# Attention with a mixture-of-experts gate: transposing through DRAM and 32x32 blocks on VectorE in place of DMA transposes

## The chip, the cores and the metric

The kernel runs on one core of one Trainium2 chip. Its engines are TensorE (PE in the profile; PEld is its weight load), VectorE (DVE), ScalarE (ACT), GpSimd (POOL) and SyncE (SP). SP computes nothing: it only issues DMAs. ACT and POOL issue DMAs too, between their computations. Each engine runs its own instructions strictly in order, so an instruction that waits holds up everything behind it on that engine. The metric is the device time in microseconds; lower is better.

## What is computed

The input `x` is 2 x 2048 rows of 512 floats, all in float32. Cut to what matters:

```python
xn = layernorm(x)
# attention branch, causal, one head of 512
z = layernorm(xn) * gamma + beta
q, k, v = z @ qkv[:, :512], z @ qkv[:, 512:1024], z @ qkv[:, 1024:]
s = softmax(mask(q @ k.T / sqrt(512))) @ v @ o_proj + xn
# mixture of experts: 8 experts, each token goes to its best 2, hidden size 352
comb = softmax over the top 2 of (xn @ gate_w.T + gate_b + bias)
h = silu(xn @ w1[e].T + b1[e])
y = h @ w2[e].T + b2[e]
g = silu(sum over the two experts of comb * y)
out = x + s * g
```

## The kernel before

TensorE contracts over the partitions, so both operands of a product need the contracted index on the partitions. Rows arrive with tokens on the partitions. Four times per token something has to be turned: the normalised rows `z` (for keys and queries), the gathered rows `xs` of a tile of 128 tokens that go to one expert, that tile's hidden values `h`, and the softmax numerators `pT`.

**How the kernel turns.** It uses the DMA transpose, which moves 2-byte elements. POOL first splits each float32 tile into its low and high 16-bit halves (`zu`, L347; `hu`, L1166; `pu`, L1495). SP issues the DMA transpose (`zuT`, L354; `xhT`, L1041; `huT`, L1170; `puT`, L1501). VectorE then joins the halves into float32 (L374, L1046, L1175, L1517). The rows for the gather are stored to DRAM in split form, so `xs` needs no copy by POOL. Only the first block of `z` and the short rows of `pT` are turned by TensorE.

**The stages.** One stage follows the other, with their edges interlaced by hand:

1. 0 to about 250 us: normalisation of 8 blocks of 512 rows, folded weights, keys, queries and values, and routing. Routing ends with `toki`, the list of tokens for each expert tile; the gathers wait for it.
2. About 250 to 570 us: the expert tiles. Tiles 0 to 6 and those from 59 on go one by one (`experts_step`, L1210). Tiles 7 to 58 go in 26 pairs (`pair_step`, L1243), where seven half-products stand for eight (`up_pair`, L1122).
3. About 570 us to the end: attention over 32 query tiles, long ones in pairs with the same seven-product scheme, and the output.

**A pair step.** The order is written out by hand, and each engine gets its part in that order. In `pair_step(i)`: ACT copies out an earlier result and SP stores it (`keep_y`, L1201); POOL gathers tile i+6; SP turns tiles i+4 and i+5 (`turn`, L1039); VectorE joins tiles i+2 and i+3 (`join_x`); `up_pair(i)` makes seven products on TensorE, which VectorE adds into `h`; between the fourth and the fifth product VectorE joins the turned hidden values of tile i-2 (`join_h`, L1173), and ACT applies Silu to them; then ACT scales the two new `h` and they are turned (`turn_h`, L1162); POOL gathers tile i+7; `join_h(i-1)`; TensorE multiplies tiles i-3 and i-2 by w2 (`down`, L1186); VectorE forms the sums for the next pair (`x_sums`, L1110). So a turned `h` is joined one pair step after it was scaled, and on VectorE that join stands ahead of the last four additions of the next pair.

**Buffers.** `xs` has 7 tiles, `xhT` 4, `huT` 3, products 5 PSUM banks (pool `ps_a`), results of `down` 3 (`ps_b`).

**Attention.** `exponentials(s)` (L1478) computes a tile's numerators piece by piece on ACT; each piece of up to 512 columns is split by POOL and turned by SP. `join_p` (L1515) comes one step later, spread between products.

Of the kernel before, what the change touches and what calls it, by code (L numbers as in the profile page):

```python
# [20 lines left out]
P = 128  # L21
# [5 lines left out]
def gated_attention_moe(  # L27
# [67 lines left out]
    ZW = 2 * D + 32  # L95
    zu_d = dram.tile([NT * P, ZW], U16, name="zu_d")
# [4 lines left out]
    zu_rows = zu_d.rearrange("(n p) d -> p n d", p=P)  # L101
    y_rows = y_d.rearrange("(n p) d -> p n d", p=P)
# [55 lines left out]
    zup = right(norm_a, name="zup", bufs=3)  # L158
# [4 lines left out]
    zus = [zup.tile([P, ZW], U16, name=f"zu_{i}", tag=f"zu_{i}", bufs=1) for i in range(BT)]  # L163
    for zu in zus:
        nc.gpsimd.memset(zu[:, 2 * D :], 0)
# [23 lines left out]
    def load_small():  # L189
        nc.sync.dma_start(out=gam, in_=gamma)  # L190
        nc.sync.dma_start(out=bet, in_=beta)
        nc.sync.dma_start(out=gw[:, :, :E], in_=gate_wt.rearrange("(c p) e -> p c e", p=P))
        for c, (h0, hn) in enumerate(HCH):
            nc.sync.dma_start(out=b1s[:hn, c, :], in_=b1_t[h0 : h0 + hn, :])
        nc.sync.dma_start(out=gb[:, :, 0], in_=gate_b.to_broadcast([P, E]))
        nc.sync.dma_start(out=gbias[:, :, 0], in_=gate_bias.to_broadcast([P, E]))
# [129 lines left out]
    def norm_rows(b):  # L326
# [3 lines left out]
        for t in range(BT):  # L330
            z = zp.tile([P, D], F32, name=f"z_{b}_{t}", tag="z")
            nc.vector.tensor_scalar(  # L332
                z, xt[:, t, :], mv[:, t, 0:1], rs[:, t, 1:2], ALU.subtract, ALU.mult
# [11 lines left out]
        for t in range(BT):  # L345
            zu = zus[t]
            nc.gpsimd.tensor_copy(  # L347
                zu[:, : 2 * D].rearrange("p (h d) -> p h d", h=2),
                zs[t].bitcast(U16).rearrange("p (d h) -> p h d", h=2),
            )  # L350
            nc.gpsimd.tensor_copy(zu[:, 2 * D : 2 * D + 2], ratio[:, t, :].bitcast(U16))
            if b >= BY_TE:
                zuT = zup.tile([P, 2 * ND, P], U16, name=f"zuT_{b}_{t}", tag="zuT", bufs=BT + 2)
                nc.sync.dma_start_transpose(out=zuT, in_=zu[:, : 2 * D])  # L354
                zuts[b, t] = zuT
        for t in range(BT):
            nc.sync.dma_start(out=zu_rows[:, b * BT + t, :], in_=zus[t])
# [4 lines left out]
    def keys(b):  # L362
# [9 lines left out]
        else:  # L372
            for t in range(BT):
                nc.vector.tensor_copy(  # L374
                    zT[:, :, ts(t, P)].bitcast(U16).rearrange("p c (t h) -> p c t h", h=2),
                    zuts.pop((b, t)).rearrange("p (h c) t -> p c t h", h=2),
                )
# [574 lines left out]
    full_rows = (NH - 1) * P  # L952

    def load_w2(e):
        nc.sync.dma_start(
            out=w2[:, e, : NH - 1, :],
            in_=w2_t[e, :full_rows, :].rearrange("(c p) d -> p c d", p=P),
        )
        nc.sync.dma_start(out=w2[:HL, e, NH - 1, :], in_=w2_t[e, full_rows:, :])
# [4 lines left out]
    xhp = st.enter_context(tc.tile_pool(name="xhp", bufs=4))  # L964
# [3 lines left out]
    def gather(i):  # L968
        xs = xsp.tile([P, ZW], U16, name=f"xs_{i}", tag="xs")
# [61 lines left out]
    hus = []  # L1031
    for i in range(NHU):
        hu = htp.tile([P, 2, NH * P], U16, name=f"hu_{i}", tag=f"hu_{i}")
        nc.gpsimd.memset(hu[:, :, H:], 0)
        nc.gpsimd.memset(hu[:, 1, H : H + 1], 0x3F80)
        hus.append(hu)
    xhs, xts, phs, huTs, hts, experts = {}, {}, {}, {}, {}, {}

    def turn(i):  # L1039
        xh = xhp.tile([P, 2 * ND, P], U16, name=f"xhT_{i}", tag="xhT")  # L1040
        nc.sync.dma_start_transpose(out=xh, in_=xss[i][:, : 2 * D])  # L1041
        xhs[i] = xh

    def join(i):
        xT = xtp.tile([P, ND, P], F32, name=f"xT_{i}", tag="xT")
        nc.vector.tensor_copy(  # L1046
            xT.bitcast(U16).rearrange("p c (t h) -> p c t h", h=2),
            xhs.pop(i).rearrange("p (h c) t -> p c t h", h=2),
# [113 lines left out]
    def turn_h(i):  # L1162
        h = phs[i] if i in paired else hp.tile([P, H], F32, name=f"h_{i}", tag="h")
        nc.scalar.mul(h, phs.pop(i), xss.pop(i)[:, 2 * D : 2 * D + 2].bitcast(F32))
        hu = hus[i % NHU]
        nc.gpsimd.tensor_copy(  # L1166
            hu[:, :, :H], h.bitcast(U16).rearrange("p (d h) -> p h d", h=2)
        )
        huT = hp.tile([P, 2 * NH, P], U16, name=f"huT_{i}", tag="huT", bufs=3)
        nc.sync.dma_start_transpose(out=huT, in_=hu.rearrange("p h d -> p (h d)"))  # L1170
        huTs[i] = huT

    def join_h(i):  # L1173
        ht = hp.tile([P, NH, P], F32, name=f"ht_{i}", tag="ht", bufs=3)
        nc.vector.tensor_copy(  # L1175
            ht.bitcast(U16).rearrange("p c (t h) -> p c t h", h=2),
            huTs.pop(i).rearrange("p (h c) t -> p c t h", h=2),
# [65 lines left out]
    def pair_step(i):  # L1243
# [3 lines left out]
        for k in range(2):  # L1247
            turn(i + 4 + k)
# [6 lines left out]
        for k in range(2):  # L1255
            turn_h(i + k)
# [85 lines left out]
    def fast_scores(s, pools, meanwhile=()):  # L1342
# [7 lines left out]
        (c11, c12), (c21, c22) = ([turned[s + i][:, ts(j, TB)] for j in range(2)] for i in range(2))  # L1350
# [3 lines left out]
        def made(x, y):  # L1354
# [7 lines left out]
            return ps  # L1362
# [115 lines left out]
    def exponentials(s):  # L1478
# [4 lines left out]
        for j, (src, at) in enumerate(pieces):  # L1483
            end = at + src.shape[1]
            nc.scalar.activation(  # L1485
                turned[s][:, at:end], src, AF.Exp, bias=nm, accum_out=rs[:, j : j + 1]
            )
# [453 lines left out]
```

## Time and profile before

| | |
|---|---|
| median of 3 runs | 1007.92 us (1007.5 to 1008.66) |
| the profiled execution | 1007.83 us, its span 1006.0 us |
| TensorE busy | 999.9 us, 3924 matmuls, granted clock 1.0 |
| VectorE busy | 716.9 us |
| ScalarE busy | 403.2 us |
| GpSimd busy | 483.3 us |
| DMA | 207.96 MB; 230776 of 296647 packets are under 512 B |
| busy share of the 16 DMA engines, 281 to 520 us | 1.01 |
| DMA transposes | 28 of `zu`, 66 of `xs`, 66 of `hu`, 74 of `pu`, all issued by SP |

The span is the time between the first and last instruction; 1.83 us of the execution lie outside it. A busy time is a sum over the whole span. An engine's idle time costs nothing unless the engine that bounds the kernel waits for it. "Landing" is the time from the start of a DMA's issue to its arrival.

### The profile page before, as it was taken

What the parts mean: (1) busy time and instruction counts of PE and PEld (TensorE: products, weight loads), DVE (VectorE), ACT (ScalarE), POOL (GpSimd) and SP (SyncE); (2) the same over time, 40 slices, a digit from 0 to 9 for tenths busy, and PEclk for the clock granted to TensorE, in tenths of its full rate; (3) what the DMA queues carried; (4) which work ended last, traced back from release to release, by engine and by line L of the source; (5) the groups of instructions that cost most, each with busy time, mean ns of one, the idle gap of its engine ahead of it and who ended that gap; (6) DMA issues with size and microseconds to landing.
All of it is one profiled execution on the core that took longest, in us unless ns stands there. A gap on an engine that the chain in (4) does not pass through costs nothing. (4 is left out here: it accounts for less than half of the span.)

```text
span 1006.0 us, 13431 instructions
## 1 busy us (share of the span) xinstructions
PE 999.9 (99%) x3924; PEld 665.3 (66%) x3924; DVE 716.9 (71%) x1396; ACT 403.2 (40%) x804; POOL 483.3 (48%) x475
## 2 busy tenths in 40 slices
PE   9999999999999999999999999999999999999998
PEld 5888888874567767766753448677675544447577
DVE  6996746897887777677744579668576556878667
ACT  3344445322444454444445112232335535442241
POOL 4474564004644454444332165254557776764272
PEclk9999999999999999999999999999999999999999
DMA  8689996978999999999999576274677768753361
GB/s 293 193 264 293 329 286 258 349 249 240 202 227 220 211 208 221 217 200 222 216 218 242 164 193 147 78 206 104 183 199 239 225 200 240 207 141 86 92 165 42
DMA packets 296647, 207.96 MB, mean 207 GB/s; under 512 B 230776, under 2 KB 243832, under 8 KB 296576
## 3 DMA queue, kind: packets, MB, share of 16 engines
q1 hardware_dynamic: 282432, 163.56, 63.2%
q0 software_dynamic: 10400, 34.63, 12.5%
q10 hardware_dynamic: 3744, 8.91, 2.4%
q8 instruction: 34, 0.56, 0.2%
q14 instruction: 37, 0.30, 0.1%
HBM read 92.35 MB, written 60.03 MB: 151 GB/s over the span
## 5 line engine op out<-in xcount | busy, mean ns | idle before, releaser
L1195 PE MATMUL py<-arena,ht 128*128 (+3 forms) x396 | 176.7, 593 | 0.0
L1307 PE MATMUL ps<-k,q 128*128 128x512 f32 (+3 forms) x416 | 143.0, 495 | 0.3 <-PEq L1455 0.3
L1495 POOL COPY pu<-pT 128x1024 uint16<-128x1024 uint16 (+2 forms) x74 | 82.5, 1146 | 118.1 <-ACT pT L1485 59.1
L1166 POOL COPY hu<-h 128x704 uint16<-128x704 uint16 x66 | 61.9, 956 | 155.8 <-issue 121.7
L1195 PEld LDWEIGHTS py<-arena,ht 128*128 128x128 f32 (+3 forms) x396 | 71.8, 185 | 80.7 <-issue 76.9
L1307 PEld LDWEIGHTS ps<-k,q 128*128 128x128 f32 x416 | 74.7, 190 | 67.1 <-issue 56.5
L970 POOL DMA_INDIRECT xs<-zu_d,toki x66 | 77.6, 1176 | 70.2 <-DVE toki L791 55.6
L1181 ACT ACTIVATE ht<-ht,b1sel 128x128 f32<-128x128 f32 (+3 forms) x216 | 67.9, 380 | 88.1 <-DVE ht L1175 88.1
L1145 DVE TENSOR_TENSOR h<-p,h 128x176 f32<-128x176 f32 x182 | 55.5, 337 | 60.7 <-PE p L1138 57.2
L1678 POOL DMA_INDIRECT yg<-y_d,posi x64 | 67.4, 1053 | 36.9 <-DVE yg L1689 21.9
L1535 PE MATMUL po<-v,pT 128*128 128x512 f32 x152 | 67.9, 592 | 0.0
L347 POOL COPY zu<-z 128x1024 uint16<-128x1024 uint16 x32 | 39.9, 1245 | 55.7 <-DVE z L332 55.7
L1517 DVE COPY pT<-puT 128x1024 uint16<-128x1024 uint16 (+2 forms) x74 | 54.1, 759 | 8.8 <-DMA puT<-pu 8.6
L1485 ACT ACTIVATE pT<-pT,nm 128x1024 f32<-128x1024 f32 x14 | 16.1, 1148 | 110.3 <-DVE nm L1395 72.0
L1203 ACT COPY y<-py 128x512 f32<-128x512 f32 x55 | 32.2, 585 | 62.3 <-PE py L1195 48.4
L1485 ACT ACTIVATE pT<-ps,nm 128x512 f32<-128x512 f32 (+3 forms) x52 | 30.1, 581 | 62.5 <-DVE nm L1395 38.8
L1365 DVE TENSOR_TENSOR pT<-p,pT 128x512 f32<-128x512 f32 x49 | 32.9, 687 | 25.8 <-PE p L1359 22.1
L1535 PEld LDWEIGHTS po<-v,pT 128*128 128x128 f32 x152 | 28.6, 190 | 31.9 <-issue 30.1
L1707 POOL TENSOR_TENSOR o<-o,yg 128x512 f32<-128x512 f32 x30 | 42.0, 1398 | 14.3 <-DVE o L1699 14.1
L1699 DVE SCALAR_TENSOR_TENSOR o<-xo,xscale,o 128x512 f32<-128x512 f32 x30 | 25.9, 871 | 30.1 <-ACT o L1696 30.1
L1046 DVE COPY xT<-xhT 128x1024 uint16<-128x1024 uint16 x66 | 45.2, 712 | 2.3 <-DMA xhT<-xs 2.0
L1708 POOL TENSOR_TENSOR o<-o,xo 128x512 f32<-128x512 f32 x30 | 43.0, 1432 | 2.4
(342 smaller groups left out, 2142.9 us busy)
## 6 DMA issues: line engine op xcount, KB each, us to landing
y_d<-y SPq DMA_DIRECT2D x66, 256.0 KB, 4.4
zu_d<-zu SPq DMA_DIRECT2D x32, 264.0 KB, 2.8
kt_d<-kT SPq DMA_DIRECT2D x16, 512.0 KB, 5.9
q<-qt_d SPq DMA_DIRECT2D x32, 256.0 KB, 5.4
k<-kt_d SPq DMA_DIRECT2D x32, 256.0 KB, 4.7
v<-v_d SPq DMA_DIRECT2D x32, 256.0 KB, 5.6
xo<-in_x_dram SPq DMA_DIRECT2D x32, 256.0 KB, 3.8
x<-in_x_dram SPq DMA_DIRECT2D x30, 256.0 KB, 4.9
```

The lines of the kernel that those rows point to most:

```text
L970: nc.gpsimd.indirect_dma_start(out=xs, out_offset=None, in_=zu_d, in_offset=bass.IndirectOffsetOnAxis(ap=toki[:, order[i] : order[i] + 1], ...
L1046: nc.vector.tensor_copy(xT.bitcast(U16).rearrange("p c (t h) -> p c t h", h=2), xhs.pop(i).rearrange("p (h c) t -> p c t h", h=2),)
L1145: nc.vector.tensor_tensor(out, x, y, ALU.add)
L1166: nc.gpsimd.tensor_copy(hu[:, :, :H], h.bitcast(U16).rearrange("p (d h) -> p h d", h=2))
L1181: nc.scalar.activation(ht[:hn, c, at], ht[:hn, c, at], AF.Silu, bias=b1sel[:hn, c, j : j + 1])
L1195: nc.tensor.matmul(py[at, :], lhsT=ht[:k, c, at], rhs=rhs[n], start=(c == 0), stop=(c == NH - 1),)
L1307: nc.tensor.matmul(ps[:, :w], lhsT=aqs[seq[s] // 2][:, c, ts(t % 2, P)], rhs=aks[first + j][:, c, :w], start=(c == 0), stop=(c == ND - 1),)
L1485: nc.scalar.activation(turned[s][:, at:end], src, AF.Exp, bias=nm, accum_out=rs[:, j : j + 1])
L1495: nc.gpsimd.tensor_copy(pu[:, : 2 * w].rearrange("p (h d) -> p h d", h=2), turned[s][:, k : k + w].bitcast(U16).rearrange("p (d h) -> p h ...
L1517: nc.vector.tensor_copy(turned[s][:, k : k + w].bitcast(U16).rearrange("p (i t h) -> p i t h", t=P, h=2), puT[:, : 2 * w // P, :].rearrang ...
L1535: nc.tensor.matmul(dst, lhsT=turned[s][:, ts(k, P)], rhs=avs[first + k // BT][:, k % BT, cols], start=(start and k == k0), stop=(k == k1 - 1),
L1678: nc.gpsimd.indirect_dma_start(out=y, out_offset=None, in_=y_d, in_offset=bass.IndirectOffsetOnAxis(ap=posi[k][:, n : n + 1], axis=0),)
```

## The change

All DMA transposes go, and with them all copies that split floats into halves. In their place a tile is written to DRAM as it is, in rows of float32. It is read back by four DMAs, one for each quarter of the columns (`by_quarters`). The quarter j lands on partitions 32j to 32j+31, with each partition holding one row of every group of 32 rows. The elements are then in the right group of 32 partitions, and one VectorE `transpose` of 32x32 blocks, of 512 or 384 columns in one instruction, puts each into its place. The result has its columns in another order (32-column groups interlaced), so `b1`, `w2` and the order in which `z` and `pT` are written are permuted to match.

Who issues what: `z` rows are stored by SP as before, and the copy in DRAM now serves both the gather and the turning. `xs` is written to DRAM by POOL (`xs_d`). `h` is scaled by ACT straight into a ring of four (`hu`) and written by ACT (`h_d`). `pT` is written by ACT (`p_d`). All reads back are on SP. In the pair steps two tiles share one set of four reads, and the two `h` share one write. `w2` and `b1` are loaded by quarters too, so that each expert takes five DMAs in place of three.

The memory pools change a little: one ring of four tiles for `xs` read back (`xring`), one of four for `h` (`huT`), eight tiles for `pT` in place of five.

```diff
+    def by_quarters(dst, src):
+
+        for j in range(4):
+            nc.sync.dma_start(out=dst[ts(j, Q)], in_=src[j])
...
         for t in range(BT):
-            zu = zus[t]
-            nc.gpsimd.tensor_copy(
-                zu[:, : 2 * D].rearrange("p (h d) -> p h d", h=2),
-                zs[t].bitcast(U16).rearrange("p (d h) -> p h d", h=2),
-            )
...
+            nc.gpsimd.tensor_copy(zs[t][:, D : D + 1], ratio[:, t, :])
+            nc.sync.dma_start(out=row, in_=zs[t])
+        if b >= BY_TE:
+            zuts[b] = zup.tile([P, BT * 4, D // 4], F32, name=f"zuT_{b}", tag="zuT")
+            by_quarters(
+                zuts[b],
+                zu_d[b * TB : (b + 1) * TB, :D].rearrange("(i b) (j e) -> j b i e", b=Q, j=4),
+            )
...
     def load_w2(e):
...
+        for j in range(4):
+            n = min(NH, (H - j * NH * Q) // Q)
+            nc.sync.dma_start(
+                out=w2[ts(j, Q), e, :n, :],
+                in_=w2_t[e, j * NH * Q : (j * NH + n) * Q, :].rearrange("(c a) d -> a c d", c=n),
+            )
         nc.sync.dma_start(out=w2[HL : HL + 1, e, NH - 1, :], in_=b2[e : e + 1, :])
...
-    def turn(i):
-        xh = xhp.tile([P, 2 * ND, P], U16, name=f"xhT_{i}", tag="xhT")
-        nc.sync.dma_start_transpose(out=xh, in_=xss[i][:, : 2 * D])
-        xhs[i] = xh
+    def turn(i, n=1):
+        for k in range(i, i + n):
+            nc.gpsimd.dma_start(out=xs_d[k], in_=xss[k][:, :D])
+        by_quarters(
+            xring[:, slots(i, n)].rearrange("p n i e -> p (n i) e"),
+            xs_d[i : i + n].rearrange("n (i b) (j e) -> j b (n i) e", i=4, j=4),
+        )
 
     def join(i):
         xT = xtp.tile([P, ND, P], F32, name=f"xT_{i}", tag="xT")
-        nc.vector.tensor_copy(
-            xT.bitcast(U16).rearrange("p c (t h) -> p c t h", h=2),
-            xhs.pop(i).rearrange("p (h c) t -> p c t h", h=2),
+        nc.vector.transpose(
+            xT.rearrange("p c (i b) -> p i c b", i=4),
+            xring[:, (i + 1) % 4].rearrange("p i (c a) -> p i c a", c=ND),
         )
...
-    def turn_h(i):
-        h = phs[i] if i in paired else hp.tile([P, H], F32, name=f"h_{i}", tag="h")
-        nc.scalar.mul(h, phs.pop(i), xss.pop(i)[:, 2 * D : 2 * D + 2].bitcast(F32))
-        hu = hus[i % NHU]
-        nc.gpsimd.tensor_copy(
-            hu[:, :, :H], h.bitcast(U16).rearrange("p (d h) -> p h d", h=2)
-        )
-        huT = hp.tile([P, 2 * NH, P], U16, name=f"huT_{i}", tag="huT", bufs=3)
-        nc.sync.dma_start_transpose(out=huT, in_=hu.rearrange("p h d -> p (h d)"))
-        huTs[i] = huT
+    def turn_h(i, n=1):
+        for k in range(i, i + n):
+            nc.scalar.mul(hu[:, (k + 1) % 4, :H], phs.pop(k), xss.pop(k)[:, D : D + 1])
+        nc.scalar.dma_start(out=h_d[i : i + n].rearrange("n p e -> p n e"), in_=hu[:, slots(i, n), :])
+        by_quarters(
+            huT[:, slots(i, n)].rearrange("p n i e -> p (n i) e"),
+            h_d[i : i + n].rearrange("n (i b) (j e) -> j b (n i) e", i=4, j=4),
+        )
 
     def join_h(i):
...
+        nc.vector.transpose(
+            ht.rearrange("p c (i b) -> p i c b", i=4),
+            huT[:, (i + 1) % 4].rearrange("p i (c a) -> p i c a", c=NH),
         )
...
         keep_y(i - DOWN - 1, nc.scalar.copy)
         gather(i + FIRST)
-        for k in range(2):
-            turn(i + 4 + k)
+        turn(i + 4, 2)
...
-        for k in range(2):
-            turn_h(i + k)
+        turn_h(i, 2)
         gather(i + FIRST + 1)
         join_h(i - 1)
...
             for k in range(at, end, TB):
                 w = min(end - k, TB)
+                p_d = dram.tile([P, w], F32, name=f"p_d_{s}_{k}")
+                nc.scalar.dma_start(out=p_d, in_=turned[s][:, k : k + w])
+
+                pool, tag, n = (op, "o", 4) if s == 1 else (php, "puT", 8)
+                puT = pool.tile([P, TB], F32, name=f"puT_{s}_{k}", tag=tag, bufs=n)
+                by_quarters(
+                    puT[:, :w].rearrange("p (i e) -> p i e", i=4),
+                    p_d.rearrange("(i b) (j e) -> j b i e", i=4, j=4),
                 )
...
     def join_p(s):
         puT, k, w = halves[s].pop(0)
+        nc.vector.transpose(
+            turned[s][:, k : k + w].rearrange("p (c i b) -> p c i b", i=4, b=Q),
+            puT[:, :w].rearrange("p (i c a) -> p i c a", i=4, a=Q),
         )
```

## The prediction, made before the changed kernel ran

> **What bounds the kernel now.** I read the page's busy times first, then TensorE's waits, then the table of windows for the stage of the pair steps, then the timeline of one pair step, and the list of DMA issues last.
>
> ```profile
> PE 999.9 (99%) x3924; PEld 665.3 (66%) x3924; DVE 716.9 (71%) x1396; ACT 403.2 (40%) x804; POOL 483.3 (48%) x475
> ```
>
> TensorE (PE) is busy 999.9 of the 1006.0 us span. Its waits say the same:
>
> ```profile
> PE warm L870 <- DVE b1s L181: 1.1, 1, 1.1
> PE p L1583 <- DVE u L1600: 0.4, 1, 0.4
> PE ps L1307 <- PEq L1455: 0.3, 1, 0.3
> PE pz L370 <- ACT zT L371: 0.3, 1, 0.3
> ```
>
> That is 2.1 us in all. Matmuls in steady stretches start 429 ns (512 columns), 216 ns (256) and 149 ns (176) apart, without holes. The change removes no matmul (3924 before and after), so the time can fall by 2.1 us of waits, plus part of the 3.8 us that TensorE lacks in the last 56 us (52.21 busy): about 4 us at most. What must be judged is whether some product will now wait. The tightest place is the stage of the pair steps (columns: window, us, busy time and instructions of PE, PEld, DVE, ACT, POOL, then PE clock, DMA share, GB/s):
>
> ```profile
> 281.00:520.00 239.00, 239.00 (x1017) 164.29 (x1016) 170.01 (x378) 112.76 (x283) 106.10 (x102) 1.00 1.01 215
> ```
>
> TensorE never idles here, and the 16 DMA engines are full too (1.01). One pair step, from the timeline (start, busy time, engine, line):
>
> ```profile
> 469.81 1.36 PE L1138 MATMUL p<-w,xT 128*128 x8
> ...
> 472.75 0.55 DVE L1175 COPY ht<-huT 128x768 uint16<-128x768 uint16 x1
> ...
> 473.21 1.31 DVE L1145 TENSOR_TENSOR h<-p,h 128x176 f32<-128x176 f32 x4
> ...
> 474.27 1.07 ACT L1164 ACTIVATE h<-h,xs 128x352 f32<-128x352 f32 x2
> ...
> 474.99 1.88 POOL L1166 COPY hu<-h 128x704 uint16<-128x704 uint16 x2 [4.69 <-issue]
> 475.98 2.54 SPq L1170 DMA_TRANSPOSE huT<-hu  x2
> ...
> 479.14 1.36 PE L1138 MATMUL p<-w,xT 128*128 x8
> ...
> 482.08 0.55 DVE L1175 COPY ht<-huT 128x768 uint16<-128x768 uint16 x1
> ```
>
> The step repeats every 479.14 - 469.81 = 9.33 us. The reader should see a closed loop: `join_h` on DVE (472.75), the four additions behind it, ACT's two scalings (end 475.34), the turning of `h`, and the next step's `join_h` (482.08), which again stands ahead of four additions. Now the first `h` is turned by a POOL copy (0.94) and a transpose that lands 3.0 after its issue at 475.98, so it arrives at about 479.0, against use at 482.08: 3 us to spare.
>
> ```profile
> huT<-hu SPq DMA_TRANSPOSE x66, 3.0
> y_d<-y SPq DMA_DIRECT2D x66, 256.0 KB, 4.4
> zu_d<-zu SPq DMA_DIRECT2D x32, 264.0 KB, 2.8
> ```
>
> **What is removed.** POOL loses 61.9 us (`hu`), 82.5 (`pu`) and 39.9 (`zu`), together 184 us. SP loses 234 transposes, which held it 1.23 (`huT`, `puT`, `zuT`) to 1.84 us (`xhT`) each, some 330 us. None of this ends a TensorE wait, so I credit nothing.
>
> **What is added on SP.** Four reads for each group: 40 groups of `xs`, 40 of `h`, 74 of `pT`, 7 of `z`, so 644 reads. A plain DMA holds SP 0.38 to 0.52 us; at 0.42 that is 270 us in place of 330. SP has room; the order on it is `xs` reads, `h` reads, `y` stores. A read that waits for its write holds the `y` stores behind it. Those free the three `y` buffers, and are not due within a step.
>
> **DMA load per pair step.** From 400 to 450 us the transposes were 20217 packets of 256 B at 24 ns, i.e. 20217 x 0.024 / 16 x 9.33 / 50 = 5.7 us of each engine per step. In their place, at the measured 88 ns for 2 KB and 51 for 1 KB packets: `xs` write 256 x 88 / 16 = 1.4; `h` write (256 of 1.5 KB, 70 ns by interpolation) 1.1; `xs` read (1024 of 512 B, 30 ns) 1.9; `h` read (1024 of 384 B, 27 ns) 1.7. My estimate is 6.1. The stage stays full, so landings stay those of a loaded queue.
>
> **The `h` loop, where the cost is.** It now has two DMAs in series.
> - Fixed: 472.75 to 475.34, 2.6 us.
> - W, ACT's write of both tiles (384 KB), until landed: no row is equal. Lower bound 2.0 (the fastest 256 KB store issued by ACT, `qt_d`), upper 4.6 (`y_d` in this stage). I take 3.3, between `zu_d` (2.8) and `y_d`.
> - Four reads on SP: three issues of 0.42, then the last one's landing. Landing: nearest is `huT` at 3.0; bounds 2.0 and 4.9 (the gathers). So 4.3, from 3.3 to 6.2.
> - Two semaphore handovers, 0.3 together.
>
> Sum 2.6 + 3.3 + 4.3 + 0.3 = 10.5 us (8.2 to 13.7), against a period of 9.33. A loop longer than TensorE's work sets the period, so each of the 26 steps loses 10.5 - 9.33 = 1.17: 30 us. About 2.3 us of slack is used up once before TensorE feels it (`down` of the step needs `ht` only then), and I add 2 us for single stalls elsewhere: +30. Queued behind the waiting `join_h` on DVE are the four additions, `x_sums` and `join_x`; TensorE runs out of PSUM banks for its products (5) and waits for `ht` in `down`. If loads relax as the period stretches, the loop can't go much past 12: (12 - 9.33) x 26 = +69.
>
> A rule speaks here. The Trainium skill, "DMA: Bandwidth & Descriptors", § Anatomy of one DMA — SWDGE (gpsimd) path, prices a DMA at about 2.0 us and its bytes at 436 KB per us. Its fit is for GpSimd's queue. It gives W = 2.9 and a quarter read 2.2, so the loop is 2.6 + 2.9 + 1.3 + 2.2 + 0.3 = 9.3, exactly the period: no loss. But it prices `y_d` at 2.6, where this stage's row says 4.6 (4.4 over all), with the DMA engines full. I side with the rows, and keep the rule's result as a rival.
>
> Against the change as a whole speaks "VectorE: DVE Perf Modes", § The three transpose paths: a plain DMA that does a transpose by strides is 19 times slower than the DMA transpose. By it a `huT` would take 19 x 1.23 = 23 us, and a step would be several times longer. I don't apply it: the reads here run over 384 to 512 contiguous bytes, and the 32x32 turning is VectorE's.
>
> **The `xs` chain.** `xs` now goes through POOL's two writes (a gather holds POOL 1.0 to 1.3 us, so I take 1.2 each), landing about 4, then SP's four reads, 4.3 to 5: about 11 us from the start of the step. `join_x` uses it 7.7 us into the next step (477.52), i.e. 17 us after. Even a W of 5 leaves room. POOL has the room: two writes replace 1.88 us of copies. No cost; if the `xs` reads wait long on SP, the `h` reads behind them are late, which belongs to the same loop.
>
> **VectorE's transposes.** No row shows one. Nearest are the joins that they replace: 0.57 (`ht`) and 0.71 (`xT`) us. Below: it moves half as many elements, so 0.3. Above: the page just named gives 311 ns for 128x128, so 0.93 and 1.24 for three and four such. I take the rows, as DVE handles the same bytes. At the upper value the loop grows by 0.4, another 10 us; at the lower it loses 0.3, 7 us less. DVE is busy 170 of 239 us here, so its sum doesn't bind.
>
> **Attention, norm, start of the experts.** A `pT` piece was 1.24 (POOL) + 1.23 (SP) and 3.2 landing; now a write of 2.8 to 3.3, 1.3 of issues and 2.5 to 3. The two are about equal, and its join comes one tile later (DVE waited there for DMA only 8.6 us in all). ACT now issues 74 writes at 0.33, in its idle time (busy 40%). I put 0 to +10 us on it, most likely 1. `zuT` is four reads in place of four transposes per block, after a store of 2.8: 0 to +3. At the start of the experts, from the gathers (225.8 to 233.2) to the first joins (239.57), a write of 3 to 5 us is put in; TensorE has other products until about 247, so it is just covered; uncovered, 3 to 5 us once. `w2` takes five DMAs in place of three, in steps with room: 0.
>
> **The rivals.**
> - A, the loop binds: 1007.8 + 30 = 1038; with L from 9.6 to 12.3, about 1013 to 1080. Chance 0.58.
> - B, on the other side: the loop stays hidden, because W and the reads together land within 9.33 - 2.9 = 6.4 us (the rule's prices, 6.4). Removing 5.7 us of small packets speaks for it. Time 1007.5; chance 0.19. Above 6.4 the loss begins, below there is none.
> - C, the loop is hidden, but attention's joins or the start stall: 1007.8 + 3 to 15, centre 1014. Chance 0.18.
> - D, faster: POOL and SP are freed, and the few us at the start and the tail shrink. At most 4 us: 1004 to 1005.7. Chance 0.05. The tail speaks against it: the last `pT` was joined at 980.28 and is used at 984.35, so it isn't what TensorE waits for.
>
> **The numbers.** The profiled execution took 1007.83 us (span 1006.0), the median of the runs is 1007.92; the sums fit either. A change under 0.2% can't be told from none here. Faster 0.05, same 0.19, slower 0.58 + 0.18 = 0.76. The range from 1006 to 1080 takes in A's bounds, B and C.
>
> **What would show it.** A: the first product of a pair step comes every 10 to 11 us in place of 9.33; TensorE's waits in that stage name DVE's additions or ACT's `ht`; `join_h` waits for the DMA of `huT`; DMA share near 1.0. B: the period is 9.33 and `join_h` waits for nothing. Each term can be read: W as the landing of `h_d`, the reads' landing, the transposes' mean. I would be wrong if `xs` reads hold SP while the `h` reads stand behind, if the quarter reads (32 partitions each) land far slower than 3 us, or if VectorE's transposes cost over 1.5 us.

## The result and the profile after

The changed kernel took 1135.25 us (median of 3 runs, 1133.22 to 1139.49) against 1007.92 us: a ratio of 1.127, 95% interval 1.122 to 1.132. It is 127 us slower. The forecast was 1038, with a range to 1080. The side was right and the size was wrong by a factor of four. The profiled execution took 1133.22 us, with a span of 1131.5 us.

The busy times and TensorE's waits of the changed kernel (who waits for whom: us in total, times, longest):

```profile
PE 1035.0 (91%) x3924; PEld 677.3 (60%) x3924; DVE 638.3 (56%) x1396; ACT 406.7 (36%) x804; POOL 323.9 (29%) x367
```

```profile
PE p L1170 <- DVE h L1177: 24.8, 12, 3.7
PE py L1225 <- ACT ht L1211: 16.3, 13, 2.1
PE ph L1118 <- DMA xring<-xs_d: 12.0, 1, 12.0
PE po L1567 <- DVE pT L1549: 8.8, 3, 3.9
PE p L1615 <- DVE s L1609: 7.7, 2, 6.4
```

The other engines got their time back as planned: POOL fell by 159 us, VectorE by 79. It bought nothing, because TensorE now waits: for VectorE's additions and ACT's Silu, which stand behind the joins (the first two lines), for the first `xs` (the third), and for `pT` (the last two). Its busy time rose as well, by 35 us with the same 3924 matmuls; the last section says why for most of it.

**Where the time went.** Both kernels run the same matmuls in the same order. So the n-th matmul's start can be compared, and the growth of the lag gives a ledger by stage (worked out from the two traces; the boundaries are matmuls 1000, 1200, 2220 and 2500). The lag at the end is 124.8 us; the rest of the span's 125.5 lies behind the last matmul. The boundary at matmul 2220 cuts the last pair step: 4.7 of the 14.5 us in the row of the last single tiles still arise in that step, so the pair steps lose 60 us and the single tiles behind them 10.

| stage | lag grows by | the prediction put |
|---|---|---|
| norm and projections | 9.2 us | within "2 us elsewhere", bound +3 |
| start of the experts | 15.7 us | 0 (3 to 5 if uncovered) |
| pair steps | 55.6 us | 30 us |
| last single tiles | 14.5 us | nothing |
| attention | 29.8 us | 1 us (0 to 10) |

The stage of the pair steps after, as a row of the table of windows (the same columns as before). Between 316.30 and 587.61 us lie the starts of 25 pair steps, so their period is 271.3 / 24 = 11.3 us on the mean in place of 9.33:

```profile
316.30:587.60 271.30, 236.76 (x961) 156.90 (x960) 138.84 (x360) 102.04 (x264) 75.56 (x96) 0.97 0.82 257
```

And what happens in a step, from the timeline:

```profile
449.94 1.07 ACT L1196 ACTIVATE hu<-h,xs 128x352 f32<-128x352 f32 x2
...
450.80 1.02 POOL L996 DMA_INDIRECT xs<-zu_d,toki  x1 [5.58 <-ACT hu L1196]
...
451.04 0.40 ACTq L1197 DMA_DIRECT2D h_d<-hu  x1
...
454.57 1.90 SPq L109 DMA_DIRECT2D huT<-h_d  x4
...
457.41 0.58 POOL L1070 DMA_DIRECT2D xs_d<-xs  x1 [3.72 <-DMA xs<-zu_d,toki]
...
460.05 0.58 DVE L1205 STREAM_TRANSPOSE ht<-huT 128x384 f32<-128x384 f32 x1
...
461.97 1.80 SPq L109 DMA_DIRECT2D xring<-xs_d  x4
...
468.86 1.30 DVE L1078 STREAM_TRANSPOSE xT<-xring 128x512 f32<-128x512 f32 x2 [5.02 <-DMA xring<-xs_d]
```

Two chains leave from the same scaling. One is the predicted one: `h` is written at 451.04, read from 454.57, joined at 460.05. The other is that of `xs`: the scaling frees a buffer, POOL's gather starts (450.80), the write waits until the gather has landed (457.41), the reads wait until the write has landed (461.97), and `join_x` still waits 5.02 us for them. VectorE's waits name both, and in this order:

```profile
DVE xT L1078 <- DMA xring<-xs_d: 91.5, 25, 18.5
DVE ht L1205 <- DMA huT<-h_d: 79.5, 32, 6.2
DVE pT L1549 <- DMA puT<-p_d: 44.6, 36, 3.9
DVE zT L399 <- DMA zuT<-zu_d: 41.6, 5, 13.2
```

Each of the four kinds of turned data is late somewhere. The sizes and landings of the new DMAs, from the list of issues:

```profile
xs_d<-xs POOLq DMA_DIRECT2D x66, 256.0 KB, 4.3
...
p_d<-pT ACTq DMA_DIRECT2D x56, 256.0 KB, 2.2
puT<-p_d SPq DMA_DIRECT2D x224, 64.0 KB, 2.2
xring<-xs_d SPq DMA_DIRECT2D x104, 128.0 KB, 2.6
h_d<-hu ACTq DMA_DIRECT2D x26, 384.0 KB, 3.5
huT<-h_d SPq DMA_DIRECT2D x104, 96.0 KB, 3.7
```

### The profile page after: what moved, and what is told of

Same layout as the page of the kernel before. It is cut to its first block, busy times and chain, and to the rows that moved or that the text cites. A ratio compares the mean times of both kernels' runs of the same rounds, so it can differ in the third digit from the quotient of the medians.

```text
span 1131.5 us, 13946 instructions
## 1 busy us (share of the span) xinstructions
PE 1035.0 (91%) x3924; PEld 677.3 (60%) x3924; DVE 638.3 (56%) x1396; ACT 406.7 (36%) x804; POOL 323.9 (29%) x367
## 5 line engine op out<-in xcount | busy, mean ns | idle before, releaser
L1225 PE MATMUL py<-arena,ht 128*128 (+3 forms) x396 | 187.0, 616 | 16.4 <-ACT ht L1211 16.3
L996 POOL DMA_INDIRECT xs<-zu_d,toki x66 | 67.9, 1029 | 230.6 <-ACT hu L1196 165.2
L1078 DVE STREAM_TRANSPOSE xT<-xring 128x512 f32<-128x512 f32 x66 | 43.6, 690 | 91.7 <-DMA xring<-xs_d 91.5
L1205 DVE STREAM_TRANSPOSE ht<-huT 128x384 f32<-128x384 f32 x66 | 37.8, 572 | 79.8 <-DMA huT<-h_d 79.5
L1549 DVE STREAM_TRANSPOSE pT<-puT 128x512 f32<-128x512 f32 (+2 forms) x74 | 46.4, 638 | 48.2 <-DMA puT<-p_d 44.6
L1170 PE MATMUL p<-w1s,xT 128*128 x208 | 43.1, 332 | 24.8 <-DVE h L1177 24.8
L1070 POOL DMA_DIRECT2D xs_d<-xs x66 | 38.2, 580 | 76.5 <-DMA xs<-zu_d,toki 75.3
L1520 ACT ACTIVATE pT<-pT,nm 128x1024 f32<-128x1024 f32 x14 | 16.1, 1148 | 114.1 <-DVE nm L1426 109.4
L1118 PE MATMUL ph<-w,xT 128*128 (+1 forms) x112 | 37.9, 487 | 14.9 <-DMA xring<-xs_d 12.0
L1170 PEld LDWEIGHTS p<-w1s,xT 128*128 128x128 f32 x208 | 34.5, 199 | 28.1 <-DVE h L1177 28.0
L399 DVE STREAM_TRANSPOSE zT<-zuT 128x512 f32<-128x512 f32 x28 | 17.4, 680 | 58.0 <-DMA zuT<-zu_d 41.6
L1731 DVE SCALAR_TENSOR_TENSOR o<-xo,xscale,o 128x512 f32<-128x512 f32 x30 | 28.4, 952 | 35.3 <-ACT o L1728 35.2
```

Of the source, the lines that this page charges most:

```text
L996: nc.gpsimd.indirect_dma_start(out=xs, out_offset=None, in_=zu_d, in_offset=bass.IndirectOffsetOnAxis(ap=toki[:, order[i] : order[i] + 1], ...
L1170: nc.tensor.matmul(ps, lhsT=x[:, c], rhs=y(c).rearrange("p o h -> p (o h)"), start=(c == 0), stop=(c == ND // 2 - 1),)
L1225: nc.tensor.matmul(py[at, :], lhsT=ht[:k, c, at], rhs=rhs[n], start=(c == 0), stop=(c == NH - 1),)
L1520: nc.scalar.activation(dst, src, AF.Exp, bias=nm, accum_out=rs[:, j : j + 1])
L1549: nc.vector.transpose(turned[s][:, k : k + w].rearrange("p (c i b) -> p i c b", i=4, b=Q), puT[:, :w].rearrange("p (i c a) -> p i c a", i= ...
```

## The experiments

My theory after the result: the `xs` chain, which the prediction had let off, is the longer of two loops that both exceed 9.33 us per step. The rivals: the `h` loop alone, only longer than predicted; or the DMA queues overloaded, so that no single chain matters. Each run below was a single execution, beside a run of the kernel before (1007.5 to 1009.9 us). The ledger by stage, in us of lag gained (made as above). It scatters from run to run: the pair steps took 55.6 to 63.6 in the four runs whose edits leave the `h` and `xs` of the experts as they are (the changed kernel, p_early, w2_three, z_early), so differences of a few us in that column mean nothing.

| run | time, us | norm | start | pairs | last singles | attention |
|---|---|---|---|---|---|---|
| the changed kernel | 1135.25 | 9.2 | 15.7 | 55.6 | 14.5 | 29.8 |
| x_early | 1108.60 | 7.4 | 20.1 | 29.6 | 15.4 | 28.4 |
| h_early | 1140.34 | 8.3 | 17.3 | 67.0 | 9.8 | 30.2 |
| xh_early | 1075.83 | 6.9 | 16.1 | 8.8 | 7.4 | 28.9 |
| p_early | 1108.91 | 6.9 | 16.2 | 60.0 | 12.6 | 5.4 |
| w2_three | 1123.73 | 7.5 | 9.3 | 57.3 | 15.7 | 25.8 |
| z_early | 1130.53 | -0.2 | 16.0 | 63.6 | 15.9 | 27.4 |
| x_dry | 1068.13 | 8.5 | 9.2 | 6.1 | 8.0 | 28.6 |
| x_alone | 1081.88 | 7.3 | 8.6 | 53.2 | 5.1 | 0.0 |
| h_alone | 1053.68 | 0.7 | 16.2 | 13.9 | 14.6 | 0.0 |
| p_alone | 1033.82 | -0.4 | 0.0 | 0.0 | 0.0 | 26.4 |
| x_ahead | 1138.60 | 6.9 | 23.3 | 67.2 | 6.4 | 26.4 |
| xh_ahead | 1144.09 | 8.0 | 21.9 | 63.1 | 16.2 | 26.5 |
| x_freerun | 1128.68 | 8.2 | 28.9 | 43.2 | 8.7 | 31.5 |
| xh_freerun | 1127.15 | 7.8 | 27.1 | 44.2 | 13.8 | 26.4 |

**Waits taken away by other data: x_early, h_early, xh_early, p_early, z_early.** The edits are of one kind:

```diff
-            xs_d[i : i + n].rearrange("n (i b) (j e) -> j b (n i) e", i=4, j=4),
+            zu_d[(i % 30) * P : (i % 30 + n) * P, :D].rearrange("(n i b) (j e) -> j b (n i) e", n=n, i=4, j=4),
```

and so for `h_d`, `p_d`, and for z with `(b - 1) * TB : b * TB` in place of `b * TB : (b + 1) * TB`.

> The changed kernel with one edit: the four reads into xring take other rows (of zu_d, long written), so they wait neither for a gather nor for POOL's write. The write is still made, and all DMAs keep number and size; the expert tiles are computed from the wrong rows. The changed kernel lags the one before by 14.7 us at the first expert product, by 57 over the pair steps, by 15 over the last single tiles. Theory 1 (the h loop sets the period of a pair step): the period stays near 11.3 us, only the start's 15 us and a few of the last tiles go, so 1115 to 1122 us. Theory 2 (the chain scale, gather, write, read, join of xs sets it, since a gather can only start when the scaling seven tiles before has freed its buffer): period 9.3 to 9.7, 1055 to 1075 us. Theory 3 (the DMA engines or queues are simply overloaded, not a chain of waits): no gain over 10 us.

> The changed kernel with one edit: the four reads into huT take rows of zu_d, long written, so they don't wait for ACT's write of h. The write is still made; the products with w2 get wrong hidden values. Theory 1 (h loop): the period of a pair step falls to 9.3 to 9.7, the start's 15 us stay: 1070 to 1085 us. Theory 2 (xs chain): the period stays above 10.7, 1120 to 1135 us. Theory 3 (overload): no gain over 10 us.

> Both edits together: neither xring's nor huT's reads wait for a write; all DMAs are still made; expert results are wrong. Theories 1 and 2: all of the 86 us of the experts go, and 9 (norm) and 30 (attention) stay: about 1047 us. If one of the single edits already gives this, that chain was alone; if each gives half or less, both chains have nearly the same length and either alone keeps the period. Theory 3 (overload): above 1080.

x_early gave 1108.6, in none of the three ranges: 29.6 us remain in the pair steps, the period is about 10.4. With xs on time, the `h` loop is left alone, and it costs about what was predicted for it. h_early gained nothing (1140, above even the range for that case; the changed kernel's own runs reach 1139). Only both together take the pair steps' loss down to 8.8 us, all of it in the first two steps; from the third on they start 9.33 us apart. So both loops are too long, the `xs` loop is the longer one, and the two overlap: taking away the shorter alone shows nothing. The start and attention kept their loss in all three; the next runs look at them. xh_early came out at 1076, not at the 1047 expected, because I had put the start and the last singles on these chains too. It also speaks against plain overload. This is its window, with all the DMAs made and the data not waited for:

```profile
310.00:500.00 190.00, 187.68 (x803) 129.28 (x803) 117.40 (x305) 90.06 (x224) 64.47 (x82) 1.00 1.02 311
```

TensorE is busy 187.68 of 190 us at a DMA share of 1.02 and 311 GB/s. The DMA engines can carry this load at the old period, if nothing waits for it in a row.

> The changed kernel with one edit: the four reads into puT take rows of zu_d, long written, in place of the numerators that ACT has just written. The writes are still made; attention multiplies wrong numerators. If attention's 30 us come from the two DMAs in series (write, then read) that end after the join is due: about 1105 us. If they come from ACT, held up by 74 issues of writes, or from loaded DMA queues: above 1125.

1108.9: attention's loss falls from 29.8 to 5.4 us. It was write and read in series, not ACT's 74 issues, which are all still made.

> The changed kernel with one edit: the four reads that turn block b of z take the rows of block b-1, stored a block earlier (keys and queries are wrong). The changed kernel loses 9.2 us in the norm stage. If that is store and read in series before the first product of a block: the loss there falls under 4 us, total 1127 to 1131. If it is the load of the DMA queues: it stays at 8 to 10, 1133 to 1137.

1130.5: the norm stage's loss goes altogether (-0.2). It was store and read in series as well.

**w2_three: w2 by three DMAs for each expert.**

```diff
     def load_w2(e):
-        for j in range(4):
...
+        nc.sync.dma_start(
+            out=w2[:, e, : NH - 1, :],
+            in_=w2_t[e, :full_rows, :].rearrange("(c p) d -> p c d", p=P),
+        )
+        nc.sync.dma_start(out=w2[:HL, e, NH - 1, :], in_=w2_t[e, full_rows:, :])
```

> The changed kernel with one edit: w2 is loaded by three DMAs for each expert as before, not by five (so its rows stand in the order of before, and the expert outputs are wrong). The stall of 12 to 14 us ahead of the first expert product was there in all runs so far, with early reads or without. In the trace SP issues the last w2 DMAs there one by one, each waiting for a DMA of ACT's that holds its lane, and the first reads into xring stand behind them. If the five DMAs are the cause: the lag at the first expert product falls from 22.7 to 9 to 14 us, the total to 1121 to 1127. If it is the chain gather, write, read itself: no change at that place, 1133 to 1137.

1123.7. The lag in the first expert product (at its fifth matmul) falls from 22.7 to 10.7 us. So 10 of the 13.5 us gained there came from an edit that the prediction priced at nothing. (By matmul 1200, where the ledger's column ends, 6.4 of them are left, because xs is then late in its turn.) The waits of SP's own queue in the changed kernel, 220 to 270 us, show how:

```profile
SPq L981 <- DMA qt_d<-j: 10.9, 2, 7.3
SPq L981 <- DMA qt_d<-so: 9.6, 2, 8.7
SPq L985 <- DMA v_d<-so: 6.3, 1, 6.3
SPq L981 <- DMA v_d<-j: 4.4, 2, 3.2
```

The loads of w2 wait for stores that ACT issued: in this program, SP's and ACT's DMAs take their completion semaphores in turn from one set of eight (in the trace, numbers 100, 102 and 104 to 109 for both engines), and a DMA waits for the one that held its semaphore before. With 40 loads in place of 24, SP ran into ACT's stores, and the first reads into `xring` came out at 262.49, behind them.

**One part alone: h_alone, x_alone, p_alone.** Each is the kernel before with one part of the diff.

> The kernel before with the h part of the change alone: h is scaled into the ring, written by ACT, read by quarters and turned by VectorE, with w2 and b1 by quarters; xs, z and pT stay on DMA transposes with POOL's copies. If the h loop is what was predicted (10.5 us against a period of 9.33) and the xs chain alone makes the rest: about 30 us over the pair steps, as in the run with early xs reads (29.6), plus up to 10 at the start through the five DMAs of w2: 1035 to 1050. If the h part costs nothing as long as xs arrives on time: under 1012. If the small packets of the transposes crowd its DMAs: above 1055.

> The kernel before with the z and xs part of the change alone: z rows stored as float32 and read back by quarters, xs written by POOL and read back by quarters; h and pT on DMA transposes, w2 in three DMAs. If the xs chain alone sets a period of 10.7 or more, as the sum over two steps says (a gather starts after the scaling seven tiles back): 35 to 60 us over the pair steps, and with 8 us in the norm stage 1055 to 1080. If xs is only late because the h loop's stretched steps and DMAs delay it: under 15 us over the pair steps, 1020 to 1035.

> The kernel before with the pT part of the change alone: ACT writes the numerators, four reads on SP bring them back, VectorE turns; xs, h and z stay as before. The changed kernel loses 29.7 us in attention, 25 of which went with early reads. If that is the series of write and read in attention's own queues: 1034 to 1041. If it came from something the other parts leave behind (DMAs late from the experts): under 1025.

Their lags at the end are 45.5, 74.2 and 26.0 us; the sum, 145.7, exceeds the change's 124.8. The overlap of the loops of `h` and `xs` in the pair steps makes 11 of these 21 us (13.9 + 53.2 against 55.6), the start of the experts 9. x_alone loses 53.2 us in the pair steps on its own, which is nearly the whole loss there (its total, 1081.9, lay just above its range). h_alone loses 13.9, less than the 30 that I still expected, and 1054 was just outside its range because of 16.2 us at the start and 14.6 in the last single tiles. p_alone loses nothing before attention and 26.4 in it.

**x_dry: the xs writes and reads left out.**

```diff
+    nc.gpsimd.memset(xring, 0.5)
+
     def turn(i, n=1):
-        for k in range(i, i + n):
-            nc.gpsimd.dma_start(out=xs_d[k], in_=xss[k][:, :D])
...
+        pass
```

> The changed kernel without the xs writes and the reads into xring: a constant is turned in place of xs (the experts' results are wrong); gathers, the h part and all else stay. With early xs reads, where those DMAs are all still made, the pair steps lost 29.6 us and the h loop took 10.45 us (write to first read 2.83, issues 1.42, last read to join 3.58, join to scaling 2.60). If the h loop's length is the latency of its two DMAs alone: again 10.2 to 10.5, 25 to 31 us. If the xs DMAs in the same queues make it long: under 9.7, under 10 us over the pair steps.

The `h` loop falls to 9.74 us, just above the 9.7 named, and the loss in the pair steps to 6.1. So latency alone makes the loop about as long as the period, and the other DMAs in the queues make it longer. Its parts, as means over 22 pair steps from the traces, us:

| run | write to first read | four issues | last issue to join | join to end of scaling | sum |
|---|---|---|---|---|---|
| predicted | 3.3 | 1.3 | 3.0 | 2.6 | 10.5 |
| changed kernel | 3.51 | 1.43 | 3.80 | 2.60 | 11.37 |
| x_early | 2.83 | 1.42 | 3.58 | 2.60 | 10.45 |
| h_alone | 3.14 | 1.40 | 2.83 | 2.62 | 10.01 |
| x_dry | 2.76 | 1.42 | 2.94 | 2.60 | 9.74 |
| x_freerun, after the flood | 2.71 | 1.42 | 2.58 | 2.66 | 9.40 |

(The sums hold 0.03 from scaling to write, in the prediction's row 0.3 for handovers. The x_freerun row is told of below; it has the 20 steps from 407 us on.) The measured parts run from one scaling to the next, so their sum is the length of a step, whatever sets it: in xh_early, where nothing waits for `h`, it is 9.33 too. Whether the loop closes without slack is told by the wait at the join. VectorE waited there for `huT` in 20 of the 22 steps of the changed kernel, in all 22 of x_early, h_alone and x_dry, and in none of xh_early.

**Mending attempts: x_ahead, xh_ahead.** The loop of `xs` runs through the scaling, which frees a buffer. So let the write free it, and gather two tiles earlier:

```diff
         for k in range(i, i + n):
-            nc.gpsimd.dma_start(out=xs_d[k], in_=xss[k][:, :D])
+            nc.gpsimd.tensor_copy(shares[:, k % 8 : k % 8 + 1], xss[k][:, D : D + 1])
+            nc.gpsimd.dma_start(out=xs_d[k], in_=xss.pop(k)[:, :D])
...
-        gather(i + FIRST)
+        if i + FIRST + 2 < NM:
+            gather(i + FIRST + 2)
```

xh_ahead has `up_pair(i, lambda: None)` and `join_h(i - 2)` behind it.

> The changed kernel with xs gathered two tiles earlier in the same seven buffers: POOL copies a tile's share into a column of its own just ahead of its write, so that the buffer is free when the write has read it and not only after the scaling. Nothing is left out. If the xs chain costs what it does because a gather can't start before the scaling seven tiles back: like early reads, 1105 to 1112, period about 10.4 (the h loop). If it is the write and the read themselves that are too slow in sum: above 1125.

> The kernel with xs gathered earlier, and also join_h of a pair's first tile behind the last four additions of the next pair, so that these don't wait for h (they are what the next h needs). TensorE needs ht only in the second product with w2, 6.8 us into its step; h arrives about 5.4 us into it and takes 1.6 more for turning and Silu. If the loop through the additions sets the period: the pair steps lose under 12 us in all and the total is 1080 to 1092. If the h DMAs simply come too late for w2's product as well: 1100 to 1110, as without it.

Both failed: 1138.6 and 1144.1. In x_ahead `xs` was no longer late in the pair steps, and yet the `h` loop grew to 11.77 us. The ring of eight shares made POOL wait for the scaling of eight tiles back, so that two writes and two gathers left within 3 us of the moment in which `h` was written:

```profile
445.37 1.07 ACT L1198 ACTIVATE hu<-h,shares 128x352 f32<-128x352 f32 x2
...
446.03 0.34 POOL L1071 COPY shares<-xs 128x1 f32<-128x1 f32 x1 [7.15 <-ACT hu L1198]
446.32 0.58 POOL L1072 DMA_DIRECT2D xs_d<-xs  x1
...
446.47 0.37 ACTq L1199 DMA_DIRECT2D h_d<-hu  x1
...
457.20 0.58 DVE L1207 STREAM_TRANSPOSE ht<-huT 128x384 f32<-128x384 f32 x1 [4.95 <-DMA huT<-h_d]
```

From `h_d` at 446.47 to the join at 457.20 is 10.7 us. In the changed kernel two gathers and one write leave in that moment as well, so that this makes the loop longer is likely but not shown. A later `join_h` didn't help either, since TensorE then waits for `ht` in the products with w2.

**x_freerun, xh_freerun: is it the moment or the number?** One column of shares for each tile, so that POOL waits for no scaling at all:

```diff
-    shares = htp.tile([P, 8], F32, name="shares")
+    shares = htp.tile([P, NS], F32, name="shares")
```

> The version with earlier gathers, with one column of shares for each tile in place of a ring of eight, so that POOL waits for no scaling any more: gathers and xs writes run ahead of the pair steps as fast as their buffers allow. All DMAs are made and nothing is left out. If the h loop grew in the version before because POOL's DMAs started with the h write: the loop falls to 10.5 or less once POOL is ahead, 10 to 30 us over the pair steps, total 1080 to 1108. If the number of DMAs alone makes the h DMAs slow, or POOL's flood crowds them: 45 us or more over the pair steps, above 1120.

> The same, with join_h of a pair's first tile behind the last four additions. h then has to come by the second product with w2, about 1.5 us later than for the additions. If the h loop is the last thing that binds and is about 10 us long: under 10 us over the pair steps, total 1070 to 1085. If it is still above 11 us: as the run without the move, within 8 us.

Neither expectation held as a whole: 1128.7 and 1127.2, 43 and 44 us over the pair steps. The windows of x_freerun show why:

```profile
300.00:350.00 50.00, 35.38 (x119) 22.21 (x118) 20.13 (x44) 14.93 (x38) 38.49 (x67) 0.90 1.04 356
350.00:400.00 50.00, 37.75 (x129) 23.11 (x128) 18.10 (x47) 13.18 (x33) 32.47 (x60) 0.83 1.01 335
400.00:450.00 50.00, 47.96 (x205) 32.55 (x205) 30.26 (x79) 20.92 (x55) 0.00 (x0) 1.00 0.62 186
450.00:500.00 50.00, 49.42 (x209) 33.40 (x208) 30.10 (x78) 21.47 (x57) 0.00 (x0) 1.00 0.69 204
500.00:550.00 50.00, 50.00 (x209) 33.77 (x208) 31.68 (x83) 24.31 (x63) 0.00 (x0) 1.00 0.66 194
```

Until about 400 us POOL floods the queues with all gathers and writes (DMA share 1.01 to 1.04), and the steps take 13 to 19 us from scaling to scaling. Then POOL is done, the share falls to 0.62 to 0.69, and the steps take 9 to 10.4 us with TensorE nearly full; the last ten come every 9.33. The write of `h` tells the two stretches apart (300 to 400 us, then 410 to 570; the last number is the landing):

```profile
h_d<-hu ACTq DMA_DIRECT2D x5, 384.0 KB, 6.9
...
h_d<-hu ACTq DMA_DIRECT2D x17, 384.0 KB, 2.6
```

So the new turning of `h` can run at the old period while other DMAs are few; POOL's flood makes its chain of two DMAs too long. The work was moved, and the loss with it. No version beat the kernel before.

## Why the prediction was wrong

- **The bound and the side were right.** TensorE had nothing to win, and a wait took the place of a copy.
- **The `h` loop was right as a mechanism; its size was near, in part by luck.** With xs on time (x_early) a step took 10.45 us for the predicted 10.5, and the pair steps lost 29.6 for 30; but the write counted 2.83 for 3.3 and the last landing 3.58 for 3.0, errors that cancel. In the kernel before (h_alone) a step took 10.0 and the loss was 13.9. In the changed kernel, with both loops at work, a step took 11.37.
- **Where the error lies.** The lag is 95 us more than the 30 forecast: 30 in the pair steps, 30 in attention, 16 at the start of the experts, 10 in the single tiles behind the pairs, 9 in the norm stage. So `xs`, told of next, is the largest miss of the stage that was judged tightest, and a third of the whole. With xs on time the run still took 1108.6 us, above the range. Apart from `w2`, what the misses have in common is a write and a read in series that was taken to be hidden without a look at the slack of its join.
- **The step that failed is "The `xs` chain".** It said: about 11 us from the start of the step, use 17 us after, "No cost". Both ends were wrong. The tile turned in a step is joined ahead of the next step's first product, 7 us after its transpose is issued, not a whole step later. And the chain begins not with the step but with the scaling that frees the gather's buffer. The trace of before had shown it: the gather, the two transposes, which hold SP 5.03 us, and the join:

```profile
477.01 1.32 POOL L970 DMA_INDIRECT xs<-zu_d,toki  x1
...
480.36 5.03 SPq L1041 DMA_TRANSPOSE xhT<-xs  x2
...
487.45 1.41 DVE L1046 COPY xT<-xhT 128x1024 uint16<-128x1024 uint16 x2 [0.52 <-DMA xhT<-xs]
```

  VectorE waited there now and then. In all it had (total, times, longest):

```profile
DVE xT L1046 <- DMA xhT<-xs: 2.0, 3, 0.8
```

  Where the landing of a transpose is on record (12 of the 52 paired tiles), the tile had come 0.02 to 1.8 us before its join, 1.0 on the mean. So the slack was about 1 us, not the 6 of the prediction (17 less 11). The sum that should have been made runs over two steps (scaling, gather, turning, join, scaling). These are means for tiles 18 to 52, in us, the first from the start of the scaling:

| | scaling to gather | gather to write (before: to transpose) | write to first read | four issues | to the join | join to scaling | two steps |
|---|---|---|---|---|---|---|---|
| before | 2.74 | 5.32 | | | 4.53 | 6.08 | 18.67 |
| after | 0.86 | 5.82 | 4.01 | 1.36 | 4.22 | 6.28 | 22.55 |

  The removed POOL copies give back 1.9 us and the second DMA costs 5.1 (4.01 + 1.36 + 4.22 - 4.53). The sums themselves are two steps long in both kernels (18.67 is 2 x 9.33), whatever sets the step, so they don't show that this chain sets it. That is shown by the join's 91.5 us of waits for `xring`, by x_early, which takes about half of the loss away, and by x_alone, which has 53.2 us of it alone.
- **Attention** was put at 1 us because two sums looked equal. The landings were even below their price: 2.2 for the write, 2.2 for the reads. What the sum lacked is SP's turn. Up to eight pieces come in a row, about 1 us apart, and each takes SP 1.4 us for its four issues, behind the wait for its write. So from the issue of a write to its first read it took 4.3 us in the median of the 74 pieces (2.0 to 11.9). With the medians of the issues and of the landing that makes 7.8, against 4.4 from the start of POOL's copy to the landing before. p_early shows that the series of write and read costs 24 of the 30 us. In SP's own waits from 690 us on, that series is the largest:

```profile
SPq L109 <- DMA p_d<-pT: 158.2, 25, 24.7
```

  Before, a transpose followed a copy by POOL; now a read follows a landing, and while SP waits for it, nothing behind it is issued. I had compared the two sums piece by piece and not looked at the queue or at the slack of the join.
- **The start**: "w2 takes five DMAs in place of three, in steps with room: 0" failed. I counted SP's time and not whom the DMAs wait for; 10 us (w2_three).
- **The norm stage** had 0 to +3 us and lost 9.2. The store landed in 4.0 us, where 2.8 was read, and the reads in 4.4; with the reads freed from the store the loss is gone (z_early).
- **The last single tiles** weren't in the sum at all: 10 us behind the last pair step, and h_alone has 13 there by itself. There each tile has a write and four reads of its own, and I had only looked at the pair steps.
- **Removed time** was rightly credited with nothing, and VectorE's transposes were rightly priced by the joins:

```profile
L1078 DVE STREAM_TRANSPOSE xT<-xring 128x512 f32<-128x512 f32 x66 | 43.6, 690 | 91.7 <-DMA xring<-xs_d 91.5
L1205 DVE STREAM_TRANSPOSE ht<-huT 128x384 f32<-128x384 f32 x66 | 37.8, 572 | 79.8 <-DMA huT<-h_d 79.5
L1549 DVE STREAM_TRANSPOSE pT<-puT 128x512 f32<-128x512 f32 (+2 forms) x74 | 46.4, 638 | 48.2 <-DMA puT<-p_d 44.6
```

  690 and 572 ns (the mean behind the busy time), against 712 and 568 of the joins.
- **The rules.** The Trainium skill's price for a DMA ("DMA: Bandwidth & Descriptors", § Anatomy of one DMA) gave 2.9 for the `h` write and a loop of 9.3, no loss. From the write to the first read it took 2.71 in x_freerun after the flood, where the loop was 9.40 and nearly nothing was lost, 2.76 in x_dry, and 3.51 in the changed kernel, where the loop exceeded the period. So the rule comes near where other DMAs are few, and I was right not to use it for this stage. The trap of the 19-fold slower transpose ("VectorE: DVE Perf Modes", § The three transpose paths) is told there of copies with a large innermost stride at the destination; it didn't show: the reads landed in 2.2 to 3.7 us (the prediction's 23 us also took SP's hold of 1.23 for the transpose's 3.0). The 311 ns of that page are for a 2-byte type, which the prediction left out; for float32 the rows above decide.
- **A sign that didn't come.** The prediction named `xs` reads that hold SP while the `h` reads stand behind. In the pair steps this happened once, in the first; after it SP had issued the `xs` reads at least 1.6 us before it could issue the first `h` read.
- **What stays open.** How much of the `h` loop's growth from 9.74 to 11.37 us comes from the moment and how much from the number of the xs DMAs. x_dry and x_freerun show that they lengthen it; a version with their number and another phase wasn't tried. The changed kernel's own steps point to the moment: in the 12 where the last `xs` read was issued up to 1.0 us after the `h` write, the write took 3.98 us to the first read on the mean, in the other 13 it took 3.00. That goes together; no run shows that one causes the other.

## What to carry to other kernels

When a copy or a one-step move is replaced by a write and a read of memory, look for the loop that holds each of them: from the event that frees its buffer, through all waits, to the next such event, and count over how many steps it runs. The slack must be read at both ends from the trace (here: about 1 us at the join), not from the start of a step; and of several loops it is the longest that shows, so that mending a shorter one shows nothing (h_early). The sum of a loop's parts is the step by construction; only a wait inside the loop tells that it binds. Count also the DMAs that merely became more: here they waited for those of another engine (w2_three), or for their turn on SP (attention).

## What the runs showed of the hardware

**TensorE's clock can halve at a short wait.** This is where most of the 35 us of additional busy time belong. From the timeline of the changed kernel, six products before a wait of 1.96 us and six after it:

```profile
444.77 2.74 PE L1225 MATMUL py<-arena,ht 128*128 x6
...
449.48 4.27 PE L1225 MATMUL py<-arena,ht 128*128 x6 [1.96 <-ACT ht L1211]
```

The trace's record of the granted clock stands at 0.50 from 450.7 for 3.4 us. There are 12 such stretches in the changed kernel, of 3.4 us or about twice or four times that, 61.6 us together, the last of them at its very end; the kernel before has only the one at its end. The other 11 begin within or just behind a wait of 1.8 to 12 us. The 83 matmuls that start in these stretches have records that are 24 us longer in sum than those of the same matmuls before; all others together are 6 us longer. So the slow clock makes 24 of the 35 us; the rest isn't explained. The Trainium skill ("TensorE: Matmul & The Clock Gate", § Part 1: The HAM clock gate) tells of half speed after an idle window of about 3.4 us. Here waits of 1.96 and 1.85 us were enough in two cases (449.5, 538.8), while waits of 3.00 and 2.98 us (483.0, 581.8) brought no such stretch. So a wait can cost TensorE more than its length, and its length alone doesn't tell whether it will; none of the prediction's cases had that.

**The busy share of the DMA engines doesn't tell how late a DMA lands.** In xh_early it was 1.02 and TensorE lost nearly nothing in the pair steps, because nothing waited for a landing. During the flood of x_freerun it was 1.01 to 1.04, and a step took up to twice as long, because each step waits for two landings in a row. And in h_alone, at 0.95 (310 to 500 us), the last `h` read was joined 2.83 us after its issue, in the changed kernel, at 0.82, only after 3.80. The changed kernel has the writes and reads of `xs` in addition, but the small packets of the transposes no longer; which of its DMAs delay the reads isn't shown.
